# Column maxima and weighted sums turned by VectorE and DMA instead of TensorE, in an attention and mixture-of-experts layer in fp32

## The chip, the cores and the metric

The kernel runs on one core of a Trainium2 chip. The metric is the device time of one execution in microseconds (us). Names of engines as in the profile: PE is TensorE, PEld its weight loads, DVE is VectorE, ACT is ScalarE, POOL is GpSimd, SP is SyncE, which here only issues DMAs.

## What is computed

4096 tokens of width 256, all in fp32: one causal attention of a single head over all tokens, then a layer of 8 experts of which each token uses two, both with a layernorm ahead and the input added back.

```python
def attention(x, Qw, Kw, Vw):               # x is the layernorm of the tokens
    scores = (x @ Qw) @ (x @ Kw).T / sqrt(256) + causal_mask
    return softmax(scores) @ (x @ Vw)

def ffn(x, W_in, b_in, W_gate, b_gate, W1, b1, W2, b2, W_out, b_out):
    h = x @ W_in + b_in
    probs = softmax(h @ W_gate + b_gate)
    topv, topi = top_k(probs, 2); topv = topv / sum(topv)
    mid = relu(einsum('nd,edh->neh', h, W1) + b1)      # computed for the chosen experts
    eout = einsum('neh,ehd->ned', mid, W2) + b2
    moe = sum over the two chosen experts of topv * eout
    return moe @ W_out + b_out

x = x + attention(layernorm(x)); x = x + ffn(layernorm(x))
```

## The kernel before

**Tiling.** P = 128 partitions. Tokens are in 8 blocks of TB = 512 (NB = 8, TPB = 4 tiles of 128), queries in 16 blocks of QB = 256 (KU = 2 tiles of 128). ND = 2 is the width of 256 in halves.

**Attention** (about 0 to 540 us). The loop over g = 0 to 15 takes a query block at a time. In the round of g it first gives out `scores(g + 1)` and then `attend(g)`, so that the scores of the next block are computed while the exponentials of this one go on. Scores are kept transposed: keys on the 128 partitions, queries along the row. `scores` (L539) makes, for every chunk c of 256 keys, a PSUM tile `ps` by eight products (L555), has ACT copy it into a tile `s` of SBUF (L564), and has DVE keep a running maximum `mx` (L570); at the end the maximum over all key tiles is in `top`, 128 x 256: for each query (column) there are still 128 partial maxima, one on each partition.

The softmax wants one maximum for each column, on every partition. `finish` (L594) makes it: two transposes by PE of `top` into `pt` (L598), a reduction by DVE along the row into `m`, 128 x 2 (L603), two more transposes by PE of `m` spread over a row of 128, into `pmax` (L608), which leaves each query's maximum on all partitions. Then, for every chunk, DVE subtracts it from `s` (L612, the diagonal chunk L618) and ACT takes the exponential (L615, L621). `attend` (L625) multiplies the exponentials by the values (L633 `po`), divides, adds to `xb` and takes the statistics of the second layernorm (`bn`, L254).

`finish` of block g + 1 is called in the middle of `attend(g)`, by the dictionary `between`: after which chunk c of keys which further work is given out. For g < CALM = 4 it is called at once, ahead of `attend(g)`; later after chunk min(g - 2, 4).

Other work of this phase stands in the same queues. `project` (L506) makes the queries `qT` of the next token block through PSUM tiles `pq` (copied by DVE), `values` (L521) its values through `pv` (copied by ACT), `enter` and `route` (L353, L386) do the input product, the gate and the choice of experts. `turn_todo` (L323) transposes a normalized token block without PE: DVE transposes in place, which turns each square of 32 x 32 by itself (two instructions of 128 x 512), and 16 DMAs on SP put the squares in their places (L334; `zT` for the first layernorm, `z1T` for the second). With `fill`, such steps are interleaved with the maxima of `scores`.

**Experts** (540 to 1031 us): tokens' rows are fetched by expert, multiplied by both weight matrices, and the results written to `parts` in DRAM, two rows for a token. The change does not touch this phase.

**Tail** (1031 to 1070 us), per token block b: `collect(b)` loads the two rows of each token (`yp`, two loads of four tiles together; blocks 0 to 5 before the last `contribute`, 6 and 7, which wait for the last results, after it); `add_up(b)` weighs and adds them into `acc`, by ACT (L1175) and DVE (L1177); `gather(b)` transposes `acc` by PE into `pa` (8 transposes, L1195), and ACT copies the two `pa` into `aT` (L1200); `leave(b)` multiplies by W_out (8 products `pf`, L1209; in fp32 each shows as two records of PE), DVE adds the residual into `ot` (L1217), and SP writes the output (L1219, L1222). The loop calls `gather(b + 1)` before `leave(b)`:

```python
    aT = gather(0)
    for b in range(NB):
        following = gather(b + 1) if b + 1 < NB else None
        leave(b, aT)
        aT = following
```

**What sets the order.** Every engine runs its instructions in the order of its list. A scheduler makes these lists from the order in which the code gives out the work and from what depends on what, except where `keep_in_program_order` or `pin` hold an instruction in its place. DMAs issued on SP take turns at eight semaphores, so that each waits for the landing of the one eight before it.

**Buffers.** PSUM: `ps_mm` 4 (ps, pq, pf), `ps_tr` 2 (pt, pmax, pa), `ps_o` 2 (po, pv). SBUF: 24 tiles `s`, which the tail's `acc` and `aT` use too.

Of the kernel before, what the change touches and what calls it, by code (L numbers as in the profile page):

```python
# [10 lines left out]
F32 = mybir.dt.float32  # L11
I32 = mybir.dt.int32
AF = mybir.ActivationFunctionType
# [24 lines left out]
def preln_attention_moe_kernel(  # L38
# [67 lines left out]
    slots = dram.tile([NE * R, LINE], I32, name="slots")  # L106
    bias1 = dram.tile([NE * P, NF], F32, name="bias1")
    parts = dram.tile([TOPK * S, D], F32, name="parts")


    zeros = const.tile([P, P], F32, tag="zeros", name="zeros")
# [208 lines left out]
            for q in range(P // SQ)  # L320
        ]

    def turn_todo(zT, z):  # L323

        def stand(i):
            on = z[:, ts(i, TPB // 2), :]
            return nc.vector.transpose(on, on)

        def move():
            for q in range(P // SQ):
                for f in range(P // SQ):
# [202 lines left out]
    KU = QB // P  # L536
    QPB = TB // QB

    def scores(g, fill=()):  # L539

# [6 lines left out]
        for c in range(g + 1):  # L547
            ps = ps_mm(f"ps{g}_{c}")
            s = piece(f"s{g}_{c}", KU, QB)
            ss.append(s)  # L550
            for u in range(KU):
                kt = c * KU + u
                lo = u * P if c == g else 0
                for d in range(ND):
                    nc.tensor.matmul(  # L555
                        ps[:, u * QB + lo : (u + 1) * QB],
                        lhsT=zT[kt // TPB][:, kt % TPB, d, :],
                        rhs=qT[b][:, d, q * QB + lo : (q + 1) * QB],
                        start=(d == 0),
                        stop=(d == ND - 1),  # L560
                    )
            flat = s.rearrange("p u q -> p (u q)")
            if c < g:
                nc.scalar.copy(flat, ps)  # L564
                if c == 0:
                    mx = flat
                else:
                    old = mx
                    mx = attn.tile([P, TB], F32, tag="mx", name=f"mx{g}_{c}", bufs=2)
                    done = nc.vector.tensor_tensor(mx, ps, old, ALU.max)  # L570
                    for do in fill[len(fill) * (c - 1) // parts_of : len(fill) * c // parts_of]:
                        if done:
                            tc.keep_in_program_order(done)
                        done = do()
                    if fill and done:
                        tc.keep_in_program_order(done)
                continue
            for u in range(KU):
                on = slice(u * P, (u + 1) * P)
                nc.vector.tensor_tensor(  # L580
                    s[:, u, on], ps[:, u * QB + u * P : u * QB + (u + 1) * P], mask, ALU.add
                )
                if u + 1 < KU:
                    nc.scalar.copy(s[:, u, (u + 1) * P :], ps[:, u * QB + (u + 1) * P : (u + 1) * QB])
            if mx is None:
                nc.vector.tensor_copy(top, s[:, 0, :])
            else:
                nc.vector.tensor_tensor(top, mx[:, :QB], mx[:, QB:], ALU.max)
                nc.vector.tensor_tensor(top, top, s[:, 0, :], ALU.max)
            for u in range(1, KU):  # L590
                nc.vector.tensor_tensor(
                    top[:, u * P :], top[:, u * P :], s[:, u, u * P :], ALU.max
                )
        def finish(behind=False):  # L594

            pt = ps_tr(f"pt{g}")
            for u in range(KU):
# [8 lines left out]
            pm = ps_tr(f"pmax{g}")  # L606
            for u in range(KU):
                nc.tensor.transpose(pm[:, ts(u, P)], m[:, u : u + 1].to_broadcast([P, P]), ident)  # L608
            for c in range(g + 1):
                s = ss[c]  # L610
                if c < g:
                    nc.vector.tensor_tensor(  # L612
                        s, s, pm[:, :QB].unsqueeze(1).to_broadcast([P, KU, QB]), ALU.subtract
                    )
                    nc.scalar.activation(s, s, AF.Exp)  # L615
                    continue
                for u in range(KU):
                    nc.vector.tensor_tensor(  # L618
                        s[:, u, u * P :], s[:, u, u * P :], pm[:, u * P : QB], ALU.subtract
                    )  # L620
                    nc.scalar.activation(s[:, u, u * P :], s[:, u, u * P :], AF.Exp)  # L621

        return ss, finish

# [454 lines left out]
    for g in range(NT // KU):  # L1079
# [18 lines left out]
        if q == 0 and b > 0:  # L1098
# [3 lines left out]
                lg = enter(b - 1, z1T, attn, behind)  # L1102

            if b - 1 >= EASY[1]:
                between[5] = [partial(send, True)]
        if q == 0 and b == NB - 1:

            def fetch_first():
# [4 lines left out]
                nonlocal seen  # L1113
                seen = route(b - 1, lg, seen, attn, True)

            between[6], between[11] = [fetch_first], [find]
            weighed = AHEAD
        elif g == 0:
            turn(0, 1, ahead, zT[1])
# [30 lines left out]
                    do()  # L1150

    HT = TPB // 2
    yps, accs = {}, {}

    def collect(b):

# [10 lines left out]
                    tc.add_to_no_dep_group("out", get.ins)  # L1167
            yps[b, i] = yp

    def add_up(b):  # L1170
        for i in range(2):
            acc = accs[b, i] = piece(f"acc{b}_{i}", HT, D)
            for j in range(HT):
                t = b * TPB + i * HT + j
                pin(nc.scalar.mul(acc[:, j, :], yps[b, i][:, j, 0, :], share[0][:, t : t + 1]))  # L1175
                pin(
                    nc.vector.scalar_tensor_tensor(  # L1177
                        acc[:, j, :],
                        yps[b, i][:, j, 1, :],
# [4 lines left out]
                    )  # L1184
                )

    def gather(b):

        pts = [ps_tr(f"pa{b}_{c}") for c in range(ND)]
        if b > 0:  # L1190
            add_up(b)
        for i in range(2):
            for j in range(HT):
                for c in range(ND):
                    nc.tensor.transpose(  # L1195
                        pts[c][:, ts(i * HT + j, P)], accs[b, i][:, j, ts(c, P)], ident
                    )
        aT = [piece(f"aT{b}_{c}", TB) for c in range(ND)]
        for c in range(ND):
            nc.scalar.copy(aT[c], pts[c])  # L1200
        return aT

    def leave(b, aT):
        for i in range(2):
            ot = piece(f"ot{b}_{i}", HT, D)
            for j in range(HT):
                pf = ps_mm(f"pf{b}_{i}_{j}")
                for c in range(ND):
                    nc.tensor.matmul(  # L1209
                        pf[:, :D],  # L1210
                        lhsT=aT[c][:, ts(i * HT + j, P)],
                        rhs=wout_sb[:, c, :],
                        start=(c == 0),
                        stop=(c == ND - 1),
# [13 lines left out]
    for n, item in enumerate(work):  # L1228
# [70 lines left out]

# [30 lines left out]
```

## Time and profile before

| what | value |
|---|---|
| timed runs: median of 3 (least, most) | 1080.48 us (1079.9, 1081.41) |
| the profiled execution, by itself | 1071.75 us |
| span of its profile, first to last instruction | 1070.0 us |
| granted clock of PE in it | 1.00 |
| busy: DVE, ACT, POOL | 674.6, 332.4, 236.9 us |
| on DVE: a subtraction of 128 x 512; a transpose of 128 x 512 | 0.68, 0.70 us |
| exponential of 128 x 512 on ACT | 0.63 us |
| 16 DMAs of one `z1T`, first to last issue; each to landing | 10.4 us; 2.0 us |
| DMA load of 512 KB of `yp`, issue to landing (least, median, most) | 5.3, 7.0, 8.7 us |
| weighing a row in the tail: ACT, DVE | 0.50, 0.48 us |

The page has the busy time of each engine and the span in 40 slices; the chain of waits goes back from the last instruction to what released it at each step. A group's row names line, engine, operation, output and inputs, shape and count. Its mean is the duration of one instruction; where instructions follow each other in a pipeline, the distance of their starts (the pace) is shorter than the duration, and for PE it is the pace that counts. The timed runs and the profiled execution are different executions: the profiled one was 8.7 us below the median.

### The profile page before, as it was taken

What the parts mean: (1) busy time and instruction counts of PE and PEld (TensorE: products, weight loads), DVE (VectorE), ACT (ScalarE), POOL (GpSimd) and SP (SyncE); (2) the same over time, 40 slices, a digit from 0 to 9 for tenths busy, and PEclk for the clock granted to TensorE, in tenths of its full rate; (3) what the DMA queues carried; (4) which work ended last, traced back from release to release, by engine and by line L of the source; (5) the groups of instructions that cost most, each with busy time, mean ns of one, the idle gap of its engine ahead of it and who ended that gap; (6) DMA issues with size and microseconds to landing.
All of it is one profiled execution on the core that took longest, in us unless ns stands there. A gap on an engine that the chain in (4) does not pass through costs nothing.

```text
span 1070.0 us, 15770 instructions
## 1 busy us (share of the span) xinstructions
PE 1062.3 (99%) x4973; PEld 882.9 (83%) x4973; DVE 674.6 (63%) x2114; ACT 332.4 (31%) x730; POOL 236.9 (22%) x289
## 2 busy tenths in 40 slices
PE   9999999999999999999999999999999999999998
PEld 6788888888888888888888887777778787777887
DVE  5877667564655546254665724858588786767636
ACT  2232233322432323242402221232323332323254
POOL 2104043103103000201222522232322322313110
PEclk9999999999999999999999999999999999999999
DMA  9422211121011011001655475887889896969285
GB/s 313 104 54 44 58 25 51 17 54 24 6 45 25 8 21 39 3 1 21 202 170 180 124 248 180 280 266 268 279 269 315 262 333 213 335 211 327 77 300 187
DMA packets 177995, 158.80 MB, mean 148 GB/s; under 512 B 82158, under 2 KB 157875, under 8 KB 177909
## 3 DMA queue, kind: packets, MB, share of 16 engines
q1 hardware_dynamic: 168980, 139.67, 42.4%
q0 software_dynamic: 8384, 17.58, 5.1%
q8 instruction: 40, 0.66, 0.3%
q10 hardware_dynamic: 544, 0.52, 0.1%
q14 instruction: 47, 0.38, 0.1%
HBM read 124.79 MB, written 26.38 MB: 141 GB/s over the span
## 4 chain that ended last, share of the span: by engine, by line
PE 97%; DVE 2%; POOL 0%; DMA 0%; issue 0%; SPq 0%; ACT 0%; DVEq 0%; POOLq 0%
PE po L633 21%; PE ps L555 21%; PE pm_a L921 11%; PE pe_a L988 11%; PE pe_b L988 5%; PE pm_b L921 5%; PE ph L362 3%; PE pm_c L951 3%; PE pf L1209 3%; PE pe_c L988 3%; PE pq L511 3%; PE pv L526 2%; PE pe_d L988 2%; PE pm_d L951 2%; PE pm_z L921 1%; PE pe_z L988 1%
## 5 line engine op out<-in xcount | busy, mean ns | idle before, releaser
L633 PE MATMUL po<-v,s 128*128 128x257 f32 x1056 | 237.9, 380 | 0.0
L555 PE MATMUL ps<-qT,zT 128*128 128x256 f32 x1088 | 233.3, 374 | 0.0
L555 PEld LDWEIGHTS ps<-qT,zT 128*128 128x128 f32 x1088 | 203.1, 190 | 28.0 <-issue 1.0
L633 PEld LDWEIGHTS po<-v,s 128*128 128x128 f32 x1056 | 197.2, 190 | 26.7
L564 ACT COPY s<-ps 128x512 f32<-128x512 f32 x120 | 70.2, 585 | 171.9 <-PE ps L555 132.6
L988 PE MATMUL pe_a<-w_a,mid_a 128*128 128x256 f32 x544 | 121.6, 380 | 0.0
L921 PE MATMUL pm_a<-hT_a,w_a 128*128 128x256 f32 x544 | 120.0, 379 | 0.0
L988 PEld LDWEIGHTS pe_a<-w_a,mid_a 128*128 128x128 f32 x544 | 102.6, 190 | 19.0 <-issue 5.6
L570 DVE TENSOR_TENSOR mx<-ps,mx 128x512 f32<-128x512 f32 x91 | 62.9, 691 | 83.7 <-ACT s L564 82.9
L930 ACT ACTIVATE mid_a<-pm_a,c_a 128x256 f32<-128x256 f32 x136 | 64.2, 472 | 165.1 <-PE pm_a L921 150.4
L921 PEld LDWEIGHTS pm_a<-hT_a,w_a 128*128 128x128 f32 x544 | 103.4, 190 | 14.1
L615 ACT ACTIVATE s<-s 128x512 f32<-128x512 f32 x120 | 72.2, 630 | 100.2 <-DVE s L612 100.2
L901 DVE STREAM_TRANSPOSE hT_a<-h_a 32x128 f32<-32x128 f32 x272 | 82.2, 302 | 3.8
L443 POOL DMA_INDIRECT slots<-assign,ati x64 | 62.5, 977 | 77.5 <-DVE ati L441 58.7
L612 DVE TENSOR_TENSOR s<-s,pmax 128x512 f32<-128x512 f32 x120 | 73.0, 679 | 7.3 <-PE pmax L608 7.3
L997 POOL DMA_INDIRECT parts<-y_a,slot_a x34 | 34.2, 1005 | 167.4 <-DVE y_a L996 138.0
L893 DVE STREAM_TRANSPOSE mid_c<-raw_c 32x256 f32<-32x256 f32 x128 | 55.8, 436 | 1.9
L988 PE MATMUL pe_b<-w_b,mid_b 128*128 128x256 f32 x256 | 56.8, 380 | 0.0
L921 PE MATMUL pm_b<-hT_b,w_b 128*128 128x256 f32 x256 | 56.6, 379 | 0.0
L988 PEld LDWEIGHTS pe_b<-w_b,mid_b 128*128 128x128 f32 x256 | 48.5, 190 | 9.4 <-issue 2.8
L921 PEld LDWEIGHTS pm_b<-hT_b,w_b 128*128 128x128 f32 x256 | 48.6, 190 | 6.6
L930 ACT ACTIVATE mid_b<-pm_b,c_b 128x256 f32<-128x256 f32 x64 | 30.1, 470 | 63.0 <-PE pm_b L921 63.0
(280 smaller groups left out, 1163.5 us busy)
## 6 DMA issues: line engine op xcount, KB each, us to landing
w_a<-in_L_ffn_W_dram SPq DMA_DIRECT2D x68, 512.0 KB, 6.0
w_d<-in_L_ffn_W_dram SPq DMA_DIRECT2D x48, 512.0 KB, 6.8
w_c<-in_L_ffn_W_dram SPq DMA_DIRECT2D x32, 512.0 KB, 8.1
w_b<-in_L_ffn_W_dram SPq DMA_DIRECT2D x32, 512.0 KB, 7.8
rows<-hr SPq DMA_DIRECT2D x16, 512.0 KB, 3.2
yp<-parts SPq DMA_DIRECT2D x14, 512.0 KB, 7.0
x<-in_L_attn_x_dram SPq DMA_DIRECT2D x7, 512.0 KB, 4.2
z1T<-z SPq DMA_DIRECT2D x112, 32.0 KB, 2.0
```

What stands on the lines that cost most here:

```text
L443: put = nc.gpsimd.indirect_dma_start(out=slots, out_offset=bass.IndirectOffsetOnAxis(ap=ati[:, j : j + 1], axis=0), in_=assign[:, TOPK * ( ...
L555: nc.tensor.matmul(ps[:, u * QB + lo : (u + 1) * QB], lhsT=zT[kt // TPB][:, kt % TPB, d, :], rhs=qT[b][:, d, q * QB + lo : (q + 1) * QB], ...
L564: nc.scalar.copy(flat, ps)
L570: done = nc.vector.tensor_tensor(mx, ps, old, ALU.max)
L612: nc.vector.tensor_tensor(s, s, pm[:, :QB].unsqueeze(1).to_broadcast([P, KU, QB]), ALU.subtract)
L615: nc.scalar.activation(s, s, AF.Exp)
L633: nc.tensor.matmul(po[u][:, : D + 1], lhsT=ss[c][:, k, ts(u, P)], rhs=vb[kt // TPB][:, kt % TPB, :], start=(kt == 0), stop=(kt == g * KU + u),
L893: pin(do())
L901: pin(do())
L921: nc.tensor.matmul(pm[:, :SB], lhsT=w1[c][:, ts(f, P)], rhs=hT[:, c, :], start=(c == 0), stop=(c == ND - 1),)
L930: nc.scalar.activation(mid[f // 2][:, f % 2, :], pm[:, :SB], AF.Relu, bias=c1[:, f : f + 1])
L988: nc.tensor.matmul(pe[ts(j, rest), :D], lhsT=mid[f][:, ts(u, P)][:, ts(j, rest)], rhs=w2[f // (NF // 2)][:, f % (NF // 2), :], start=(f == 0),
```

## The change

In ten query blocks (5 to 14), `scores` itself now makes the columns' maxima, in `spread_top`: DVE transposes `top` in place in squares of 32 x 32, reduces each group of 32, moves the four groups of partitions beside each other by four copies, reduces these, and has the 256 maxima written to a small DRAM tile `tops`; a second DMA reads them back onto all 128 partitions. `finish` subtracts that `top`, in SBUF, in place of `pmax` in PSUM. Blocks 0 to 4 and 15 go as before (`top_by_pe`). `finish` of the ten is given out after chunk min(g - 1, 6).

In the tail the sums of token blocks 3, 5 and 7 are added up into one tile (`add_up_apart`), transposed in place by DVE, and put in place by 16 DMAs, eleven on SP and five on POOL (`turn_sums`, through `turn_todo`); `leave` multiplies from that tile. Blocks 0, 1, 2, 4 and 6 keep their transposes by PE. The loads of `yp` come in the order 0, 3, 1, 2, 5, 4 and then 7, 6. In place of 1832 listed instructions PE has 1781, DVE 1264 for 1236, ACT 665 for 671, POOL 231 for 228, and SP 903 for 880.

```diff
-    def turn_todo(zT, z):
+    def turn_todo(zT, z, queues=(nc.sync,)):
...
-                    nc.sync.dma_start(
+                    queues[(q * P // SQ + f) % len(queues)].dma_start(
...
-    def scores(g, fill=()):
+    def scores(g, fill=(), far=False):
...
+        def spread_top():
+
+            nc.vector.transpose(top, top)
+            m4 = attn.tile([P, QB // SQ], F32, tag="m4", name=f"m4_{g}", bufs=2)
+            nc.vector.tensor_reduce(
+                m4, top.rearrange("p (b k) -> p b k", k=SQ), AX.X, ALU.max
+            )
+            c4 = attn.tile([SQ, P // SQ, QB // SQ], F32, tag="c4", name=f"c4_{g}", bufs=2)
+            for k in range(P // SQ):
+                nc.vector.tensor_copy(c4[:, k, :], m4[ts(k, SQ), :])
+            m = attn.tile([SQ, QB // SQ], F32, tag="m1", name=f"m1_{g}", bufs=2)
+            nc.vector.tensor_reduce(m, c4.rearrange("p k b -> p b k"), AX.X, ALU.max)
+            home = tops[g % 2 : g % 2 + 1, :]
+            nc.sync.dma_start(out=home.rearrange("o (b i) -> (o i) b", i=SQ), in_=m)
+            nc.sync.dma_start(out=top, in_=home.to_broadcast([P, QB]))
+
+        if far:
+            spread_top()
+
         def finish(behind=False):
-
-            pt = ps_tr(f"pt{g}")
...
+            pm = top if far else top_by_pe(behind)
             for c in range(g + 1):
...
-            nxt, finish = scores(g + 1, fill)
+            far = CALM <= g < NT // KU - 2
+            nxt, finish = scores(g + 1, fill, far)
             if g < CALM:
                 finish()
             else:
-                between[min(g - 2, 4)] = [partial(finish, True)]
+                between[min(g - 1, 6) if far else 4] = [partial(finish, True)]
...
+    EARLY = [0, 3, 1, 2, 5, 4]
...
+    def add_up_apart(b, keep=tc.keep_in_program_order):
+
+        home = attn.tile([P, TPB, D], F32, tag=f"z{b // 2 % 2}", name=f"sum{b}", bufs=1)
+        add_up(b, home, keep)
+        accs[b] = home
+
+    def turn_sums(b):
+        tag, bufs = ("z1T", 1) if b == NB - 1 else ("qT", 2)
+        aT = attn.tile([P, TPB, ND, P], F32, tag=tag, name=f"aT{b}", bufs=bufs)
+        for do in turn_todo(aT, accs[b], (nc.sync, nc.gpsimd, nc.sync)):
+            done = do()
+            if done:
+                tc.keep_in_program_order(done)
+        turned[b] = aT.rearrange("p j c t -> p c j t")
+
     def gather(b):
 
+        if b in turned:
+            return turned.pop(b)
         pts = [ps_tr(f"pa{b}_{c}") for c in range(ND)]
-        if b > 0:
+        if b > 1:
             add_up(b)
...
-            for b in range(NB - LATE):
+            for b in EARLY:
                 collect(b)
             add_up(0)
+            add_up_apart(3, pin)
         contribute(item, got.pop(n), mid)
...
-    for b in range(NB - LATE, NB):
+    aT = gather(0)
+    turn_sums(3)
+    add_up(1, None, tc.keep_in_program_order)
+    for b in (7, 6):
         collect(b)
-
-    aT = gather(0)
     for b in range(NB):
         following = gather(b + 1) if b + 1 < NB else None
+        if b in (1, 3):
+            add_up_apart(b + 4)
         leave(b, aT)
+        if b in (1, 3):
+            turn_sums(b + 4)
         aT = following
```

More of the change, by code (lines that the diff above doesn't have):

```diff
@@ L108, in preln_attention_moe_kernel @@
     parts = dram.tile([TOPK * S, D], F32, name="parts")
+    tops = dram.tile([2, QB], F32, name="tops")
     zeros = const.tile([P, P], F32, tag="zeros", name="zeros")
@@ L593, in scores, with top_by_pe @@
                 )
-        def finish(behind=False):
+        def spread_top():
[14 more added lines that the diff above has]
+            spread_top()
+        def finish(behind=False):
+            pm = top if far else top_by_pe(behind)
+            for c in range(g + 1):
+                s = ss[c]
+                if c < g:
+                    nc.vector.tensor_tensor(
+                        s, s, pm[:, :QB].unsqueeze(1).to_broadcast([P, KU, QB]), ALU.subtract
+                    )
+                    nc.scalar.activation(s, s, AF.Exp)
+                    continue
+                for u in range(KU):
+                    nc.vector.tensor_tensor(
+                        s[:, u, u * P :], s[:, u, u * P :], pm[:, u * P : QB], ALU.subtract
+                    )
+                    nc.scalar.activation(s[:, u, u * P :], s[:, u, u * P :], AF.Exp)
+        def top_by_pe(behind):
             pt = ps_tr(f"pt{g}")
@@ L608, in finish @@
                 nc.tensor.transpose(pm[:, ts(u, P)], m[:, u : u + 1].to_broadcast([P, P]), ident)
[L609 to L621, printed above, removed]
+            return pm
         return ss, finish
@@ L1104, in preln_attention_moe_kernel @@
             if b - 1 >= EASY[1]:
-                between[5] = [partial(send, True)]
+                between.setdefault(5, []).append(partial(send, True))
         if q == 0 and b == NB - 1:
@@ L1114, in find @@
                 seen = route(b - 1, lg, seen, attn, True)
-            between[6], between[11] = [fetch_first], [find]
+            for c, do in ((6, fetch_first), (11, find)):
+                between.setdefault(c, []).append(do)
             weighed = AHEAD
@@ L1152, in preln_attention_moe_kernel @@
     HT = TPB // 2
-    yps, accs = {}, {}
+    EARLY = [0, 3, 1, 2, 5, 4]
+    assert NB - LATE == len(EARLY)
+    yps, accs, turned = {}, {}, {}
     def collect(b):
@@ L1168, in collect, with add_up @@
             yps[b, i] = yp
-    def add_up(b):
+    def add_up(b, home=None, keep=pin):
         for i in range(2):
-            acc = accs[b, i] = piece(f"acc{b}_{i}", HT, D)
+            acc = piece(f"acc{b}_{i}", HT, D) if home is None else home[:, ts(i, HT), :]
+            accs[b, i] = acc
             for j in range(HT):
                 t = b * TPB + i * HT + j
-                pin(nc.scalar.mul(acc[:, j, :], yps[b, i][:, j, 0, :], share[0][:, t : t + 1]))
-                pin(
+                keep(nc.scalar.mul(acc[:, j, :], yps[b, i][:, j, 0, :], share[0][:, t : t + 1]))
+                keep(
                     nc.vector.scalar_tensor_tensor(
@@ L1197, in gather @@
                     )
-        aT = [piece(f"aT{b}_{c}", TB) for c in range(ND)]
+        aT = [piece(f"aT{b}_{c}", TPB, P) for c in range(ND)]
         for c in range(ND):
-            nc.scalar.copy(aT[c], pts[c])
+            nc.scalar.copy(aT[c].rearrange("p j t -> p (j t)"), pts[c])
         return aT
     def leave(b, aT):
+        dma = not isinstance(aT, list)
         for i in range(2):
@@ L1210, in leave @@
                         pf[:, :D],
-                        lhsT=aT[c][:, ts(i * HT + j, P)],
+                        lhsT=aT[:, c, i * HT + j, :] if dma else aT[c][:, i * HT + j, :],
                         rhs=wout_sb[:, c, :],
```

## The prediction

> **What bounds the kernel now.** I read the engine totals first, then the chain of waits, then TensorE's list of waits:
>
> ```profile
> PE 1062.3 (99%) x4973; PEld 882.9 (83%) x4973; DVE 674.6 (63%) x2114; ACT 332.4 (31%) x730; POOL 236.9 (22%) x289
> PE 97%; DVE 2%; POOL 0%; DMA 0%; issue 0%; SPq 0%; ACT 0%; DVEq 0%; POOLq 0%
> PE pt L598 <- DVE top L589: 1.0, 1, 1.0
> PE pf L1209 <- ACT aT L1200: 0.6, 1, 0.6
> ```
>
> TensorE (PE) is busy for 99% of the span and makes up 97% of the chain; its waits after the start come to under 4 us over the whole kernel. So each TensorE instruction taken away is worth its full pace, and each new wait of TensorE costs its full length. There is no slack to hide one in. What a transpose really takes shows in the timeline around query block 6 (start, length, engine, line):
>
> ```profile
> 129.37 0.38 PE L598 MATMUL pt<-ident,top 128*128 128x128 f32 x2
> 129.58 1.03 PE L633 MATMUL po<-v,s 128*128 128x257 f32 x4
> 129.79 0.42 DVE L603 TENSOR_REDUCE m<-pt 128x2 f32<-128x256 f32 x1 [2.37 <-PE pt L598]
> 130.45 0.38 PE L608 MATMUL pmax<-ident,m 128*128 128x128 f32 x2
> 130.67 1.69 PE L633 MATMUL po<-v,s 128*128 128x257 f32 x7
> 130.87 1.28 DVE L612 TENSOR_TENSOR s<-s,pmax 128x512 f32<-128x512 f32 x2 [0.66 <-PE pmax L608]
> ```
>
> The group's 273 ns is a modelled end; the starts say 129.37 to 129.58 for two pt and 130.45 to 130.67 for two pmax: 0.43 us in all. The old way was already laid between two products, so DVE and PE waited for nothing else.
>
> **What the skill says.** The Trainium skill, "VectorE: DVE Perf Modes", "The three transpose paths": VectorE's transpose turns 32x32 blocks alone, which is why the change needs copies or DMAs after it; the trace has the same pair already for z1T (a stream transpose, then 16 DMAs). "DMA: Bandwidth & Descriptors", "Anatomy of one DMA": about 2 us of each DMA is fixed, mostly the receipt. The trace agrees: 2.0 us for z1T, the least, middle and longest 2.0, 2.0 and 2.1. The same page, "Issuing engines are not separate DMA queues": spreading DMAs over queues saves issue time alone; no run here shows it yet.
>
> **Part A, ten query blocks (5 to 14).** Removed from PE: 4 transposes each, 10 x 0.43 = 4.3 us. Added, per block: one DVE transpose of 128x256, a reduce, four copies, a small reduce (together about 1.5 us, an estimate from 0.70 us for a 128x512 transpose and 0.42 us for reduce m), and two dependent DMAs on SP. For the latter two I take 2.0 us each as for z1T, to 3.7 us for the 128 KB broadcast read (the trace's c_a). The maximum is thus ready some 6 us after the last top, against 1 us before; attend(g) stands between and covers it, in most blocks by more. DVE's in-order queue is what matters: the subtractions (0.61 us each at pace) are placed one to two groups later, behind other work of DVE, and ACT's exp and PSUM copies stand behind them. Block by block, from where top was ready, where the subtractions began before, and the new order on DVE and SP:
> - Block 5: top ready 93.4; SP is issuing 16 z1T DMAs from 87.8 to 98.2, so the maxima are written at about 100.2 and read back at 102.3 to 104. DVE gets to the subtractions at 104.0 (98.3 before). The new order lets ACT do one exp before the copy of the values pv_0 and three before that of pv_1, and PE needs those two PSUM buffers for pv_2 and pv_3. Exp at 104.0 + 0.78, for 0.63, the copy 0.37: the buffer is free at 105.8, and PE wants it at 105.07 (its start of pv at 103.74 less 0.43, and two pv of 0.87): 0.8 late. Three more exps at 0.605 and a copy of 0.37: 108.0, wanted at 107.6. Stall 1.2, up to 3 if the read lands later.
> - Block 7: subtractions at about 163.2 (156.9 before); x and the layernorm statistics now precede them, and pv, qT and pk come late by 0.4, 0.3 and 0.2 us less overlaps. Stall 0.75.
> - Block 6: landing 134.5 to 135, DVE there at 135.4; its last running maximum comes 1 us before it is needed. Stall 0. Blocks 8 to 14: landings well ahead, subtractions within +5 us of before in long groups. Stall 0 to 0.1 together.
> Sum of A: -4.3 + 1.2 + 0.75 + 0.1 = -2.2 us. Without the cover of attend(g), each block would cost some 6 us; the part lives from it.
>
> **Part B, the tail.** The period of one token block in the tail (timeline of PE):
>
> ```profile
> 1039.78 2.76 PE L1209 MATMUL pf<-wout,aT 128*128 128x256 f32 x12
> 1042.38 0.38 PE L1195 MATMUL pa<-ident,acc 128*128 128x128 f32 x2
> 1042.60 0.60 PE L1209 MATMUL pf<-wout,aT 128*128 128x256 f32 x2
> 1043.03 0.60 PE L1195 MATMUL pa<-ident,acc 128*128 128x128 f32 x4
> 1043.47 0.60 PE L1209 MATMUL pf<-wout,aT 128*128 128x256 f32 x2
> 1043.90 0.38 PE L1195 MATMUL pa<-ident,acc 128*128 128x128 f32 x2
> 1044.12 1.25 PE L1209 MATMUL pf<-wout,aT 128*128 128x256 f32 x5
> ```
>
> 1044.12 - 1039.78 = 4.34 us, of which 16 pf records are 16 x 0.217 = 3.47 and 8 pa are 0.87. Three blocks lose their pa: -2.6 us. ACT loses six copies (0.59 us), worth nothing, as ACT is idle most of the time.
>
> But in this listing the pa lie spread between pf. The new order loses that for blocks 4 and 6: PE does all of pf(2), then all of pa(4), then pf(3), and DVE does the four ot of block 2 and only then the four acc of block 4 (the same for 4 and 6). From the last pf record: 0.20 us to DVE's start (129.58 to 129.79 above), ot 0.42, four acc at a pace of 0.42, 0.20 to the PE and the last transposes, 0.1 to 0.2: 2.6 us until pa is done, where its own work is 0.87. Stall 1.75 each, 3.5 together. This follows from data and program order; only its size can be off, by about 0.3 each.
>
> Then the turned blocks. Each is one DVE pass of two 128x512 transposes (1.4 us), then 16 DMAs, 11 on SP and 5 on POOL. z1T's 16 took 10.4 us to issue on SP alone (0.65 each), so 11 take about 7.2 us. The transfers are in competition with the loads of yp (columns: stretch, us, then busy time with count for PE, PEld, DVE, ACT and POOL, the clock, the DMA share, GB/s):
>
> ```profile
> 1035.00:1040.00 5.00, 5.00 (x31) 4.42 (x30) 4.00 (x11) 2.74 (x7) 0.00 (x0) 1.00 1.05 361
> 1040.00:1045.00 5.00, 5.00 (x29) 4.36 (x28) 3.23 (x9) 3.38 (x8) 0.00 (x0) 1.00 0.97 337
> 1045.00:1050.00 5.00, 5.00 (x29) 4.36 (x28) 3.60 (x9) 3.33 (x9) 0.00 (x0) 1.00 1.05 369
> 1050.00:1055.00 5.00, 5.00 (x29) 4.36 (x28) 3.79 (x10) 3.33 (x9) 0.00 (x0) 1.00 0.47 162
> ```
>
> The DMA engines are full until 1050 and half free afterwards. Landings that I work out: block 3 by 1042 to 1044.6, needed 1047.5; block 5, which stands on SP behind the last yp loads and two outputs, by 1054.4 to 1056, needed 1057.1; block 7 by 1062.8 to 1064.3, needed 1064.0. So 0 to 1 us of stall, at block 7; I take 0. If the last one is late, nothing follows it but four products and the outputs, so it comes through in full. The five DMAs on POOL cost it about 1 us each (0.98 for its indirect ones), and it has nothing else to do there. That yp is loaded in another order (0, 3, 1, 2, 5, 4, then 7 before 6) moves bytes, not their sum; I cost it at nothing, as before shows no wait of ACT or DVE on a load of yp, and the loads of blocks 1 and 2 are only two places later (14 loads are issued in 10.2 us, so 1.5 us); if a wait came there, it would be of that length. Sum of B: -2.6 + 3.5 = +0.9.
>
> **Sum.** -2.2 + 0.9 = -1.3 us with the landings of A at their later end; at the earlier end its stalls are 0.6 less, -1.9. I take the middle, -1.6. The profiled execution was 1071.75 us (span 1070.0), 8.7 below the median of the timed runs, 1080.48; I carry the difference over: 1080.48 - 1.6 = 1078.9. A measurement of this kernel can tell about 0.2%, 2.2 us, from no change: the bounds are 1078.3 and 1082.6, so the forecast lies within, next to the edge of faster.
>
> **Rivals.**
> - Cover holds everywhere (the stalls of blocks 5 and 7 do not come, because PE's values and scores have other PSUM buffers to go on with, and the acc of blocks 4 and 6 cost less than 1.75). For it: ACT is busy 31%, DVE 63%, and four buffers serve the scores. Against: the order on DVE is fixed. A gives -4.1, B +0.3: -3.8, 1076.7 us.
> - Slower, one mechanism: the 16 small DMAs of blocks 5 and 7 stand on SP behind the big yp loads, and each DMA there waits for the landing of the one eight earlier. Before, the last four yp loads were issued at 1037.75 only because 7 us went by until earlier ones landed. If the turned block 5 lands at 1061 or later, not 1055, PE stands for 4 us and block 7 inherits it. From 1059 on the whole change loses. At 1061 to 1063: -1.6 + 4 to 6, about 1083.9 us.
> - The round trip through DRAM takes 3.5 us more than I take. Then block 5 stalls by 3 more, block 6 by 2.5 and block 7, which has 4 us between landing and use, by nothing more, nor do the long later ones: if all of it reaches PE, -1.6 + 5.5, 1084.4 us; DVE's other work would fill half of it: about 1081.6 us. For it: the maxima go out as 256 single elements of 4 bytes, which no transfer of before does. Against: SP is idle at most of these times.
>
> **Chances and range.** Forecast 0.48 (its own range 1077.3 to 1080.6; 0.17 of it below 1078.3, 0.31 within), first rival 0.25 (all faster), second 0.18 (all slower but 0.02), third 0.09 (0.06 slower). Faster 0.42, same 0.36, slower 0.22. The range takes in most of the first rival and the lower half of the second: 1075.0 to 1083.5.
>
> **What would show it.** Right: PE without pt and pmax at blocks 5 to 14; a wait of PE before pv of about 1 us near 105; two waits of pa on acc of about 1.7 us in the tail, at blocks 4 and 6, as the two longest of PE's list. Wrong: waits of pf on a DMA into aT5 or aT7 of over 1 us (second rival); subtractions that wait for the DMA into top (third); no waits of PE at all near 105 and 163 (first). A median below 1076 or above 1083 would mean that a term is off by more than its bounds.

## The result, and the profile after

| | before | after |
|---|---|---|
| median of the timed runs | 1080.74 us | 1122.99 us |
| ratio, 95% interval | | 1.039 (1.0377 to 1.0404) |
| span of the profile | 1070.0 us | 1121.5 us |
| last attention product (po) starts | 563.8 | 600.9 |
| last product of the experts (pe_z) starts | 1030.9 | 1072.4 |
| last product of the tail (pf) starts | 1066.4 | 1117.8 |

The kernel became 42 us slower. By the three rows of the traces, 37.1 us of the 51.4 are lost in attention, 4.4 in the experts, which the change does not touch, and 9.9 in the tail. Of the 4.4, 2.8 are the wait of pm_a in the list below, with a stretch of half clock after it. That wait goes with the chip and not with the change, as the next paragraph explains.

The profiles and the timed runs came from several chips, of two kinds: on two of the six chips whose numbers are on record the kernel before takes 1081 us, on the other four 1071.4 to 1071.6. The profile of before is from a chip of the quicker kind, its first timings and the changed kernel's runs are from one of the slower. All eight profiles of kernels other than before that were taken on the slower kind have the wait of pm_a, and none from the quicker kind has it. Every difference of times below is therefore taken against before on the same chip; this is also why the two spans differ by 9 us more than the two medians.

The engine line of the page of the changed kernel, and then its list of waits of TensorE (us in total, times, longest):

```profile
PE 1074.2 (96%) x4909; PEld 885.2 (79%) x4909; DVE 689.6 (61%) x2180; ACT 326.9 (29%) x724; POOL 245.7 (22%) x304
```

```profile
PE pv L528 <- DVE x L672: 6.4, 2, 3.5
PE ps L557 <- DVE mx L572: 6.1, 2, 3.9
PE pv L528 <- ACT v L535: 5.7, 1, 5.7
PE pf L1258 <- DMA aT<-sum: 4.7, 1, 4.7
PE ps L557 <- DVE qT L520: 3.5, 1, 3.5
PE pv L528 <- DVE past L420: 3.0, 1, 3.0
PE ps L557 <- ACT s L566: 3.0, 2, 2.0
PE pm_a L946 <- ACT mid_a L955: 2.8, 1, 2.8
PE pa L1243 <- DVE acc L1208: 2.4, 2, 1.4
```

Two things are to be seen. The span less the busy time was 7.7 us and is 47.3: TensorE stands, and in attention it stands for VectorE (x, mx, qT, past) or for ACT behind it (v, s). And its busy time rose by 11.9 us, although it has 64 records fewer. What stands behind the first is one line in VectorE's own list:

```profile
DVE s L620 <- DMA top<-tops: 88.2, 10, 14.8
```

All ten blocks made VectorE wait for the maxima to come back, 8.8 us each on average, and everything behind the subtraction in its queue waited with it. Block 5 in the timeline (start, length, engine, line):

```profile
95.12 0.20 DVE L607 TENSOR_REDUCE m<-c 32x8 f32<-32x32 f32 x1
...
98.07 0.54 SPq L609 DMA_DIRECT2D tops<-m  x1
...
103.11 1.89 PE L528 MATMUL pv<-vw,zT 128*128 128x256 f32 x8
...
104.91 0.35 SPq L610 DMA_DIRECT2D top<-tops  x1
...
109.02 3.10 DVE L620 TENSOR_TENSOR s<-s,top 128x512 f32<-128x512 f32 x5 [3.78 <-DMA top<-tops]
...
110.34 0.35 ACT L535 COPY v<-pv 128x256 f32<-128x256 f32 x1
...
110.75 2.07 PE L528 MATMUL pv<-vw,zT 128*128 128x256 f32 x4 [5.75 <-ACT v L535]
```

The maxima were ready at 95.3 and came back at 109.0. SP's queue took 2.75 us of this, the write 6.8, the read 4.1. The last row also shows where the busy time rose: four records of pv took 2.07 us, where eight of them had taken 1.89 at 103.11. The windows have the clock (third number from the end):

```profile
105.00:110.00 5.00, 0.00 (x0) 0.00 (x0) 1.22 (x4) 0.20 (x1) 0.00 (x0) 0.89 0.34 26
110.00:115.00 5.00, 4.25 (x10) 3.41 (x11) 3.34 (x8) 3.81 (x10) 1.27 (x2) 0.50 0.00 0
```

TensorE's clock fell to half while it stood: the 0.89 of the first row is half a clock from 108.9 on, and TensorE went on at 110.75, with the half clock lasting until 115.8. The trace has seven such stretches, of 3.4 or 6.8 us, 30.7 us in all. TensorE stood in 4.5 us of them, so some 13 us of work were lost, where the kernel before had no such stretch until its end. The same four times over all ten blocks, from the trace (us after the step ahead of it):

```
block   maxima ready   write issued   read issued   subtraction   together
  5         95.3          +2.8           +6.8          +4.1         13.7
  6        130.8          +5.5           +8.0          +4.2         17.7
  7        163.7          +5.7           +6.6          +4.0         16.3
  8        209.5          +1.4           +6.8          +3.7         11.8
  9        241.5          +4.0           +7.1          +3.7         14.8
 10        293.4           0.0           +6.4          +4.2         10.6
 11 to 14                  0.0       +6.2 to +6.8   +3.4 to +4.4  10.1 to 10.9
```

### The profile page after: what moved, and what is told of

It is laid out like the page before. It is cut to its first block, busy times and chain, and to the rows that moved or that the text cites. A ratio compares the mean times of both kernels' runs of the same rounds, so it can differ in the third digit from the quotient of the medians.

```text
span 1121.5 us, 15807 instructions
## 1 busy us (share of the span) xinstructions
PE 1074.2 (96%) x4909; PEld 885.2 (79%) x4909; DVE 689.6 (61%) x2180; ACT 326.9 (29%) x724; POOL 245.7 (22%) x304
## 5 line engine op out<-in xcount | busy, mean ns | idle before, releaser
L557 PE MATMUL ps<-qT,zT 128*128 128x256 f32 x1088 | 240.6, 381 | 12.5 <-DVE mx L572 6.1
L557 PEld LDWEIGHTS ps<-qT,zT 128*128 128x128 f32 x1088 | 206.7, 194 | 44.2 <-DVE mx L572 7.2
L658 PE MATMUL po<-v,s 128*128 128x257 f32 x1056 | 234.5, 380 | 0.0
L620 DVE TENSOR_TENSOR s<-s,top 128x512 f32<-128x512 f32 x95 | 58.8, 684 | 88.2 <-DMA top<-tops 88.2
```

What stands on the lines that cost most here:

```text
L557: nc.tensor.matmul(ps[:, u * QB + lo : (u + 1) * QB], lhsT=zT[kt // TPB][:, kt % TPB, d, :], rhs=qT[b][:, d, q * QB + lo : (q + 1) * QB], ...
L620: nc.vector.tensor_tensor(s, s, pm[:, :QB].unsqueeze(1).to_broadcast([P, KU, QB]), ALU.subtract)
L658: nc.tensor.matmul(po[u][:, : D + 1], lhsT=ss[c][:, k, ts(u, P)], rhs=vb[kt // TPB][:, kt % TPB, :], start=(kt == 0), stop=(kt == g * KU + u),
```

## The experiments

**Each part by itself.** The kernel with only the one or only the other half of the diff.

> Only the maxima are made in the new way, the tail is as before. Theory (round trip): from the last attention product the trace of the changed kernel is 37.1 us later than before, so this kernel takes before + 37 to 41 (the 4.4 us lost at the start of the expert phase included), if the two parts add up. Rival (tail): the late end is mostly the tail's doing, so this one is within 10 us of before.

> Only the sums of three token blocks are turned in the new way, the maxima are as before. Theory: the tail alone was 9.9 us longer in the changed kernel's trace, so before + 5 to 10. Rival (the tail was only upset because the late attention shifted the loads and DMAs in the tail): about before + 0.9, as the prediction had it.

Measured on one chip, before at 1080.78: only the maxima 1111.38 (ratio 1.0287, 1.0269 to 1.0305), only the sums 1092.41 (1.0107, 1.0089 to 1.0125). So +30.6 and +11.6, together 42.2, and the whole change has 42.3: the parts add up. The maxima fell short of the 37 that the traces of two chips had suggested, and the sums cost more than the 5 to 10 expected. The tail's loss is its own and not a consequence of the late attention.

**The work without the wait.** VectorE's part and both DMAs are done in all ten blocks, but into a tile that nothing reads; TensorE makes the maxima that are used.

```diff
-            nc.vector.transpose(top, top)
+            nc.vector.transpose(spare, top)
...
-            nc.sync.dma_start(out=top, in_=home.to_broadcast([P, QB]))
+            nc.sync.dma_start(out=spare, in_=home.to_broadcast([P, QB]))
...
-            pm = top if far else top_by_pe(behind)
+            pm = top_by_pe(behind)
```

> The maxima are made by TensorE as before, and used from there; beside it VectorE's transpose, reductions and copies and both DMAs are done too, into a tile that nothing reads. Theory (the wait costs, not the work): within 2 us of before. Rival (VectorE's added work and the two DMAs in SP's queue crowd out others): at least 10 us slower than before. If so, the wait isn't the whole cause.

Measured: 1081.79 against 1080.78, 1.0009 (1.0 to 1.0018). VectorE's added work and the DMAs cost about 1 us; the other 30 come with the use of their result. This run also leaves `finish` after the chunk where before has it, and not one or two chunks later as the change does. The next run has it later too and loses next to nothing, so what costs the 30 us is the wait for the maxima.

**The write in longer pieces.** The DRAM row of 256 maxima was written from 32 partitions with 8 each, in an order that makes 256 pieces of 4 bytes. One more transpose of 32 x 32 by VectorE turns it into 8 partitions with 32 each (`square1` is a tile of zeros with room for two such squares).

```diff
-            nc.vector.tensor_reduce(m, c4.rearrange("p k b -> p b k"), AX.X, ALU.max)
+            nc.vector.tensor_reduce(
+                square1[:, g % 2, : QB // SQ], c4.rearrange("p k b -> p b k"), AX.X, ALU.max
+            )
...
+            nc.vector.transpose(m, square1[:, g % 2, :])
...
-            nc.sync.dma_start(out=home.rearrange("o (b i) -> (o i) b", i=SQ), in_=m)
+            nc.sync.dma_start(
+                out=home.rearrange("o (b i) -> (o b) i", i=SQ), in_=m[: QB // SQ, :]
+            )
```

> As the run with only the maxima, but one more small transpose by VectorE lays the 256 maxima as 8 rows of 32, and the write to DRAM is 8 pieces of 128 bytes in place of 256 of 4 bytes. Theory (many small elements make the write slow to complete): from the issue of the write to the issue of the read 2 to 3 us in place of 6.2 to 8.0; the kernel gains at least 15 us on the one with only the maxima. Rival (the time is the fixed cost of a DMA pair, whatever its elements): 6 us or more again, and the same time as with only the maxima, plus nothing.

Measured: 1081.42 against 1080.78, 1.0001 (0.9993 to 1.001), 30 us under the run with only the maxima. From write to read it takes 1.2 to 1.6 us, less than the 2 to 3 expected. TensorE's list of waits in it:

```profile
PE ps L559 <- DVE mx L574: 4.8, 1, 4.8
PE pm_a L953 <- ACT mid_a L962: 2.8, 1, 2.8
PE pv L530 <- ACT v L537: 1.8, 1, 1.8
```

Of the waits in attention two are left, in blocks 5 (pv, at 107) and 6 (ps, at 150). With these two the part still gains nothing over before.

**Without blocks 5 and 6.** The mended way in blocks 7 to 14 only.

```diff
-            far = CALM <= g < NT // KU - 2
+            far = 6 <= g < NT // KU - 2
...
-                between[min(g - 1, 6) if far else 4] = [partial(finish, True)]
+                between[min(g - 1, 6) if far else min(g - 2, 4)] = [partial(finish, True)]
```

> Maxima by VectorE and DMA with the 8 long pieces, in blocks 7 to 14 only; blocks 5 and 6 go as before. Theory (with the write mended, what is left of the loss is made in blocks 5 and 6, where the trip waits behind the 16 DMAs on SP and where POOL's two steps of the layernorm come apart): eight blocks save 8 x 0.43 = 3.4 us with no new wait, so before - 2.5 to - 3.5. Rival (the remaining blocks pay as well): within 1 us of before.

Measured: 1067.83 against 1071.56, 0.9965 (0.9952 to 0.9979); a second reading gave 1067.73 against 1071.41, 0.9966 (0.9952 to 0.998). So 3.7 us less (2.3 to 5.1 by the interval), 0.46 for each block where the prediction took 0.43 off, and no wait of TensorE in attention is added. On chips of the quicker kind, where both readings were taken, this is faster than before; on the slower kind it was not run, so the rival of the second reading stays open.

> Long pieces in blocks 7 to 14, for a second reading. Theory: before - 3.5 to - 4 on either chip, as it keeps TensorE's maxima in block 5 and with them whatever before has there. Rival: - 7, as the nine blocks had on the 1081 chip.

**The same eight blocks, with the write as it was, and with 32 pieces.** The first has the 256 pieces again; the second writes the same 1 KB as 32 pieces of 32 bytes (each query then subtracts another one's maximum, which the division takes out). The two kernels differ in this one line.

```diff
-            nc.sync.dma_start(out=home.rearrange("o (b i) -> (o i) b", i=SQ), in_=m)
+            nc.sync.dma_start(out=home.rearrange("o (i b) -> (o i) b", i=SQ), in_=m)
```

> Maxima by VectorE and DMA in blocks 7 to 14 only, but written as in the change, 256 elements of 4 bytes. Theory (the write's slow completion alone makes the loss, also where SP's queue is free): write to read 6 us or more in all eight, TensorE waits again before scores and values at the blocks where it did in the run with ten, and 12 us or more slower than the same eight with 8 long pieces. Rival (it was blocks 5 and 6 and the queue on SP): within 2 us of the eight with long pieces.

> As the run before it in this list, but the same 1 KB is written as 32 pieces of 32 bytes, in an order of queries that the read doesn't undo, so each query has another query's maximum subtracted, which the division by the row's sum takes out again. It is run for its times. Theory (the time goes with the number of pieces): write to read between the 1.2 us of 8 pieces and the 6.2 of 256; in proportion 1.2 + 24/248 x 5 = 1.7 us, and about the time of the eight with long pieces. Rival (it is the pieces' smallness that costs): 4 us or more.

Measured, before at 1071.5: 256 pieces 1095.93 (1.0224, 1.0207 to 1.0241), 32 pieces 1067.79 (0.9966, 0.9953 to 0.9978). Block 10 on SP, where its queue was free, with 256 pieces, and then with 8:

```profile
279.79 0.33 SPq L609 DMA_DIRECT2D tops<-m  x1
286.55 0.35 SPq L610 DMA_DIRECT2D top<-tops  x1
```

```profile
263.43 0.30 SPq L614 DMA_DIRECT2D tops<-m  x1
264.65 0.35 SPq L617 DMA_DIRECT2D top<-tops  x1
```

6.8 us against 1.2 from one issue to the next; with 32 pieces 1.3 to 3.3. In the first, the trace's packets of 4 bytes had all ended by 281.5, 1.75 us after the issue: the DMA counts as landed only 5 us after its last packet, and what fills these 5 us the trace does not show. The list of the DMAs in this stretch agrees (count, KB, us to landing):

```profile
tops<-m SPq DMA_DIRECT2D x1, 1.0 KB, 6.7
```

That form of the write costs 28.1 us over eight blocks (1095.93 less 1067.79, on one chip, with nothing changed but the order in which the same bytes are laid down). VectorE waits for the maxima with either form, but not for the same time. Its list with 256 pieces, and then with 8:

```profile
DVE s L620 <- DMA top<-tops: 80.1, 8, 14.4
```

```profile
DVE s L627 <- DMA top<-tops: 32.1, 7, 7.1
```

With 8 pieces it stands for up to 7.1 us in one block, and TensorE does not stand for it. So here a wait of VectorE costs nothing by itself; it costs where it lasts longer than the work that TensorE has at hand. Whether the number of pieces or their being under 32 bytes makes it slow was not told apart.

**Block 6.** Its subtraction comes at 137 in the mended kernel, and then its running maxima wait until 149.5 behind the layernorm of `z`, which waits for two steps on POOL. Ten blocks, and then nine without block 6, on one chip.

> Ten blocks with long pieces, to stand beside the nine on one chip. Theory (POOL's two steps of the layernorm come apart in block 6, 4.8 us and half a clock stretch): slower than the eight blocks' before - 3.7; before + 1 to + 4. Rival (what its first profile showed was that chip's, not the kernel's): before - 2 to - 4.

> Long pieces in block 5 and 7 to 14; block 6 goes as before. Theory (block 6 alone breaks POOL's order; block 5 costs 1 to 2 us of wait before the values and saves 0.43): before - 2 to - 3.5 us, and at least 4 us under the ten. Rival (block 5 is what costs): like the ten.

Measured, before at 1081.06: ten blocks 1081.37 (1.0002, 0.9993 to 1.0011), nine 1073.85 (0.9928, 0.9912 to 0.9945). POOL's timeline with ten, and then with nine:

```profile
136.43 0.23 POOL L265 TENSOR_SCALAR ln1rstd<-ln1mv 128x4 f32<-128x4 f32 x1 [25.45 <-DVE ati L445]
137.14 1.41 POOL L447 DMA_INDIRECT slots<-assign,ati  x1 [0.47 <-issue]
...
147.14 0.96 POOL L447 DMA_INDIRECT slots<-assign,ati  x1 [0.31 <-issue]
148.13 1.05 POOL L266 TENSOR_TENSOR ln1rstd<-ln1rstd,half 128x4 f32<-128x4 f32 x1
```

```profile
138.95 0.23 POOL L265 TENSOR_SCALAR ln1rstd<-ln1mv 128x4 f32<-128x4 f32 x1 [27.93 <-DVE ln1mv L259]
139.27 1.04 POOL L266 TENSOR_TENSOR ln1rstd<-ln1rstd,half 128x4 f32<-128x4 f32 x1
141.34 1.08 POOL L447 DMA_INDIRECT slots<-assign,ati  x1 [1.03 <-DVE ati L445]
```

With block 6 in, eight indirect DMAs of POOL stand between the two steps, the second step comes at 148.1, and TensorE waits 5.0 us, until 150.3. Its clock is at half from 148.1 on for 6.8 us, of which it works 4.7 and so loses 2.3. 5.0 + 2.3 - 0.43 makes 6.9 us, and the two kernels are 7.5 apart. The ten came out between what the theory (+1 to +4) and the rival (-2 to -4) had said.

The nine gained 7.2 us, more than 9 x 0.43 = 3.9 and more than expected. Two kernels that keep TensorE's maxima in block 5, only the sums and the work without the wait, have on a slower chip a wait of pmax for m of 3.3 and 3.4 us near 101, with a half-clock stretch. If before has it there too, block 5 in the new way takes it away. That was not shown: three profiles of the unchanged kernel all fell on chips of the quicker kind, with spans of 1069.7 to 1069.9 us, and tell nothing of it. What is on record fits, though. On the slower kind the timed runs of before have a mean granted clock of 0.995 to 0.998, mostly 0.997, where the quicker kind has 1.000. Of 1079 us, 0.003 is 3.2 us; with the two waits of 3.3 and 2.8 us this makes 9.3, and the two kinds are 9.2 to 9.7 us apart. The nine ran on the slower kind alone and the eight on the quicker alone, so neither gain is known on the other.

> The kernel before, unchanged, for a second profile of it. Theory: the 8.7 us between its profiled execution and its timed median are two waits that the profile of every changed kernel so far has and its own has not: about 3 us near 100 us, while VectorE waits before the reduction of pt, and 2.8 us of TensorE before pm_a near 610 us, each followed by 3.4 us or more at half the clock. If they show here, the span is 1078 to 1081. Rival: they belong to the changes, and this span is near 1070 again.

> The kernel before, unchanged, once more. Two chips have served so far, one on which it takes 1071.5 us and one on which it takes 1081. Theory: where it takes 1081, its profile has the wait of pmax for m of 3.3 us near 100 us and the wait of pm_a of 2.8 us near 610 us, which the profiles of other kernels on that chip had, and half a clock stretch after each; where it takes 1071.5, neither. Rival: on the 1081 chip the profile has neither wait, and the clock is lower throughout.

> The kernel before, unchanged, a third time, for the chip on which it takes 1081 us. As for the second: there its profile has the wait of pmax for m of 3.3 us near 100 us and the wait of pm_a of 2.8 us near 610 us (theory), or neither (rival); on the other chip it says nothing.

**The tail: half of the loads.** The loads of yp bring one of the two rows of each token, which is used twice; that leaves half of the bytes out of the tail.

```diff
-                get = nc.sync.dma_start(out=yp[:, j : j + step], in_=part[:, j : j + step])
+                get = nc.sync.dma_start(
+                    out=yp[:, j : j + step, :1], in_=part[:, j : j + step, :1]
+                )
...
-                        yps[b, i][:, j, 1, :],
+                        yps[b, i][:, j, 0, :],
```

> Only the three sums turned, once more, to stand on the same chip beside the run with half the loads. Theory: before + 10 to 12, with a wait of pf for aT of about 5 us.

> Only the three sums turned, and the tail loads one of the two rows of each token (the first, used twice): half the bytes in the same number of loads. Theory (the turn's DMAs are late because the DMA engines are full with the loads until 1050): the wait of pf for aT goes to under 1 us, the share of the DMA engines from 1030 to 1050 falls to about half; 8 us or more faster than with whole loads. Rival (the DMAs are late because each waits its turn at the semaphores in SP's queue, and half of the bytes changes nothing in the number of waits): the wait stays above 3 us.

Measured, before at 1071.5: whole loads 1082.71 (1.0106, 1.0089 to 1.0123), half 1075.78 (1.0046, 1.0029 to 1.0063). The wait of pf, and the DMA engines (the share stands next to last), with whole loads and then with half:

```profile
PE pf L1231 <- DMA aT<-sum: 4.5, 2, 2.5
```

```profile
1030.00:1035.00 5.00, 4.43 (x28) 3.75 (x28) 3.80 (x10) 2.67 (x6) 3.42 (x5) 1.00 1.05 392
1035.00:1040.00 5.00, 5.00 (x31) 4.39 (x30) 3.81 (x11) 2.98 (x7) 1.57 (x3) 1.00 1.11 334
```

```profile
PE pf L1233 <- DMA aT<-sum: 0.6, 1, 0.6
```

```profile
1030.00:1035.00 5.00, 4.43 (x28) 3.77 (x27) 3.33 (x8) 2.67 (x6) 2.51 (x4) 1.00 0.52 162
1035.00:1040.00 5.00, 5.00 (x30) 4.39 (x29) 3.73 (x10) 3.06 (x7) 1.49 (x3) 1.00 0.53 79
```

With half of the bytes the wait is gone, and the first eleven DMAs on SP take 7.6 us to issue in place of 11.9. The turns in SP's queue are the same in number but not in length. With whole loads SP's own list of waits (from 1018 to 1075) has this line, and with half of them it has none such:

```profile
SPq L334 <- DMA yp<-parts: 6.0, 5, 1.9
```

So the bytes of the loads are what makes the turned blocks late, in part through SP's turns, which wait for the loads to land. By itself this run does not part the two; the next one takes the DMAs out of SP's queue. The gain is 6.9 us, a little under the 8 expected. Without that wait the tail still loses 4.3 us against before, and these were not taken apart.

**The tail: all DMAs on POOL, and the sums given out earlier.** The first gives `turn_todo` POOL alone as queue; the second calls `add_up(4)` and `add_up(6)` one block sooner.

```diff
-        for do in turn_todo(aT, accs[b], (nc.sync, nc.gpsimd, nc.sync)):
+        for do in turn_todo(aT, accs[b], (nc.gpsimd,)):
```

```diff
-        if b > 1:
+        if b == 2:
             add_up(b)
...
+        if b in (2, 4):
+            add_up(b + 2)
         leave(b, aT)
```

> Only the three sums turned, with all 16 DMAs of each issued by POOL and none by SP. Theory (the 11 DMAs on SP, each waiting for the landing of the eighth before it, hold up the last yp loads and each other): the wait of pf for aT of 5.3 us goes, and with it its half clock; 6 us or more faster than with eleven on SP. What is left over before is the two waits on acc, about 2.7 us, less 2.6. Rival (the DMA engines are full, whoever issues): the wait stays within 2 us of 5.3.

> Only the three sums turned, DMAs as in the change, but the sums of blocks 4 and 6 are given out before the products of the block ahead of the one in between. Theory: the two waits of pa on acc (1.4 us each in the trace) go; 2 to 3.5 us faster than with only the three sums turned. Rival: something else is late in their place (the loads of block 6), and the gain is under 1 us.

Measured, before at 1071.56: POOL 1080.89 (1.0089, 1.0073 to 1.0104), earlier 1082.05 (1.0098, 1.0083 to 1.0114). Beside the +11.2 of the part as it is, these are +9.3 and +10.5. On POOL the wait of pf is 4.2 us, but it now is for the first turned block (1051.7), no more for the second. The DMAs stand in no queue with the loads, and still take more than twice the 2.0 us of z1T to land while the loads go on (from 1030 to 1060; count, KB, us to landing):

```profile
aT<-sum POOLq DMA_DIRECT2D x32, 32.0 KB, 4.9
```

This is the rival: the engines are full whoever issues, though POOL's queue takes its own turns too. With the sums given out sooner, TensorE's waits for acc fell from 2.4 to 1.4 us, while the wait for aT rose from 4.5 to 5.1, and the gain is 0.7 us: the rival again.

**The whole change with the write mended.**

> The whole change, with the write alone mended (8 pieces of 128 bytes). Theory (the parts add up): the mended ten blocks by themselves, plus the 11.2 us of the tail; so 11 us over the run of the mended ten blocks in this call, and 28 to 31 us under the changed kernel. Rival (the late attention and the tail had hurt each other): 15 us or more away from that sum.

Measured: 1092.28 against 1081.06, 1.0092 (1.0075 to 1.0109): 10.9 over the ten mended blocks by themselves, 30.7 under the changed kernel, which ran on another chip of the slower kind. The sum holds.

## Why the prediction was wrong

The prediction had 1078.9 us, and 0.22 for slower. Two of its terms failed, the price of the write (some 30 us) and the time in which the turned blocks land in the tail (some 10). With the write alone mended the whole change is still 11 us slower than before, so neither term by itself would have saved the forecast. Both of the signs that it had named for being wrong came: subtractions that wait for the DMA into `top`, and a wait of pf of over 1 us for the turned block 5. By its steps:

- **What a transpose of TensorE is worth**: right. 3.4 us for eight blocks by 0.43, and 3.7 measured, once nothing waited.
- **The price of the two DMAs: this is the larger of the two steps that failed.** "For the latter two I take 2.0 us each as for z1T, to 3.7 us." The write took 6.2 to 8.0 us from its issue to that of the read, not 2.0. z1T was the wrong row to price it by: it writes SBUF in pieces of 128 bytes, and this one DRAM in 256 pieces of 4 bytes. No row of before shows such a write. The nearest is a read of 256 pieces of 4 bytes from DRAM, beside the weight loads of the experts, at 5.2 us:

```profile
slot_a<-slots SPq DMA_DIRECT2D x17, 1.0 KB, 5.2
```

  The read, 3.4 to 4.4 us until VectorE could start, was about as priced. With the write in longer pieces the first is 1.2 to 1.6 us, and 30 us of the loss are gone. The prediction named the odd form of the write, in its third rival, and yet took the row of another.
- **The third rival** had the right place and an excess of 3.5 us, where 4 to 6 were measured. Its total, 1081.6 to 1084.4, was far off because it let blocks 5 and 6 alone pay, "nor do the long later ones". The waits show that TensorE stood in blocks up to 15: VectorE takes its instructions in order, and behind the subtraction stood the running maxima of the next scores, the copies of the queries and x. A long `attend` gives TensorE products to go on with, but what stands behind VectorE's subtraction is late for the scores and values that come next. With the old write in blocks 7 to 14 alone, TensorE still stood seven times.
- **SP's queue**: seen for block 5 (98.2 forecast, 98.07), missed for its size in 6, 7 and 9, where the write stood 5.5, 5.7 and 4.0 us behind the 16 DMAs of zT or z1T.
- **Block 5's stall of 1.2 us**: with the mended write 1.8, of the mechanism named. **Block 7's 0.75**: did not show. **Block 6, "stall 0"**: wrong, 5.0 us and a stretch of half clock, through POOL's order, which the prediction had not followed there. The two timelines of POOL above show it.
- **The clock**: not in the sum at all. Seven stretches at half clock are some 13 us of the profile's 51, and "each new wait of TensorE costs its full length" was too little for those that had such a stretch after them.
- **The two waits on acc**, 1.75 each: right in kind, 1.4 and 1.0 measured.
- **The turned blocks, the other step that failed**: the second rival came true. Block 5 was to land at 1054.4 to 1056, and the rival decided from 1061; TensorE got it at 1104.12, which less the 41.5 of the late start is 1062.6:

```profile
1074.54 12.19 SPq L336 DMA_DIRECT2D aT<-sum  x11
...
1086.83 2.34 SPq L1195 DMA_DIRECT2D yp<-parts  x4
...
1091.80 10.38 SPq L336 DMA_DIRECT2D aT<-sum  x11
...
1104.12 9.57 PE L1258 MATMUL pf<-wout,aT 128*128 128x256 f32 x32 [4.66 <-DMA aT<-sum]
```

  The eleven DMAs of block 3 took 12.2 us to issue, not 7.2 as from quiet times, so the last loads went out 7.6 us later than before (1086.83 - 41.5 = 1045.3 for 1037.75), and with them all that stood behind. With half of the loads' bytes the eleven take 7.6 us, close to the forecast: the step that failed is a time to issue taken from quiet engines, used where the same prediction had found them full. This part was taken as +0.9, and is +11 to +12.
- **The carried difference of 8.7 us** between the profiled execution and the median goes with the chips, not with the executions: where both were taken on one chip, they agree within 0.2 us (1071.67, 1071.47 and 1071.54 profiled, 1071.53, 1071.48 and 1071.51 timed). It did no harm to the difference forecast.

The Trainium skill, "DMA: Bandwidth & Descriptors", "Anatomy of one DMA", is borne out in that completion and not transfer is what one waits for: 1.75 us of packets and 5 us more here. The about 2 us that the section gives as fixed are for DMAs that GpSimd issues; the prediction carried them over to SP, where z1T agreed. For the write to DRAM they hold in neither form, 6.2 to 8.0 us with 256 pieces and from 1.2 with 8, and the measurement decides. Of the same page, "Issuing engines are not separate DMA queues" agrees with the run with POOL's queue alone: the wait for aT stayed at 4.2 us.

## What to carry to other kernels

Price a DMA by a row with the same number and size of pieces and the same target, not by its bytes; if no such row exists, keep its upper end open, and write a small result as few rows rather than as single elements. Where one engine is busy for 99% of the time, having work for it during a round trip is not enough: the round trip may stop the in-order queue of another engine, so list what is queued there behind the first instruction that needs the result. And count a stall of TensorE with its aftermath: stretches of half clock followed some of them here, worth up to 1.7 us for each 3.4.

## What was not expected of the hardware

- A write of 1 KB to DRAM as 256 pieces of 4 bytes: 6.2 to 8.0 us until the read could be issued, 1.75 us of it packets; as 32 pieces of 32 bytes 1.3 to 3.3, as 8 of 128 bytes 1.2 to 2.7.
- TensorE's clock fell to half, for 3.4 or 6.8 us, with waits of 2.0 to 5.8 us, but not with each: waits of 2.2, 2.9 and 3.0 us in the same trace had none. The traces show what decides. The seven stretches of the changed kernel start at 108.93, 153.31, 187.44, 265.95, 521.95, 648.24 and 1102.21 us, which are whole multiples of 3.413 us apart. Cut the 19 traces of this case that hold records of the clock into slices of such a grid, and of the slices at full clock all 28 in which TensorE stood for 1.95 us or more have half clock in the next slice; of the 19 with 1.55 to 1.95 us, 5 do; of the 5863 with less, none. So a wait that falls across two slices can go free: the same wait of pm_a, 2.8 us, in the same kernel (ten mended blocks) had a stretch after it in one execution, with 2.3 us of it in one slice, and none in another, with 1.7.
- The same kernel took 1081 us on two chips and 1071.5 on four. On the first kind, all eight profiles have a wait of pm_a of 2.8 us between 606 and 649 us, which none from the second kind has. Why is not known.
